# Second experts stage: the last unit's routing chain kept together, its counting behind more gates, and part of the third products ahead of the branch

## The chip, the cores and the metric

The kernel runs on one core of one Trainium2 chip. The metric is device time in microseconds (us) of one execution; lower is better. The times compared are medians of runs without a profile. The traces shown come from one profiled execution each. PE is the matrix engine (TensorE), DVE is VectorE, ACT is ScalarE, POOL is GpSimd, and SP is SyncE, which here only issues DMAs.

## The reference

Four residual stages in float32 on 1024 tokens of width 256. The change touches the fourth alone.

```python
x = x + layernorm(attention(layernorm(x)))        # 16 heads, softmax
x = x + layernorm(experts_0(layernorm(x)))        # 8 experts, all tokens
x = x + layernorm(attention_1(layernorm(x)))      # 16 heads, recurrent state
x = x + layernorm(experts_1(layernorm(x)))

def experts_1(x):                                 # 16 experts, top 4
    scores = softmax(x @ gate_weight.T)
    topk_weight, topk_idx = top_k(scores, 4)
    y = 0
    for e in range(16):
        w_e = sum(where(topk_idx == e, topk_weight, 0.0), axis=-1)
        y = y + w_e[:, None] * glu(x, gate_up[e], down[e])      # hidden 176
    return y + glu(x, shared_gate_up, shared_down)              # hidden 352

def glu(x, gate_up, down):
    g, u = split(x @ gate_up.T)
    return silu(g) * u @ down.T
```

## The kernel before

The last stage runs from about 1000 us to the end. It computes 13 of the 16 experts sparsely (on the tokens routed to them) and the last three, together with the shared network, densely (on all tokens, weighted by routing weights that are zero where a token did not choose them).

*Dense part.* The hidden units of the shared network and of the three dense experts are cut into seven tiles of up to 128. `gates(i, hf, part)` computes tile `i` for half `hf` of the tokens (512), or for a quarter of them (`early`, `late`): `gated` issues the matmuls `pg` and `pu` on PE (L828), the Silu `sg` on ACT (L830) and the product `mid` on DVE (L831). Five of the seven tiles hold hidden units of the dense experts; `weighted(hf)` multiplies those with the routing weights (DVE, L1683). `spreads()` prepares these weights: PE transposes `pt` (L1613), ACT copies, a write to DRAM, and broadcast loads on SP's queue (L1623). `down(products(hf), part)` forms the third products (`po`, L846) for the half, or for one pair of its 128-token blocks ("part 1" or "part 2"), and ACT copies or DVE adds them into `acc` (L856, L853).

*Routing.* `routed(u)` is a generator in three steps for the units of 2, 2 and 4 blocks of tokens:
1. logits `pl` on PE (L1513), and then on DVE, with one exponential on ACT, the softmax and the choice of four experts: `top` (L1518) to `chosen` (L1539) and `counts` (L1544).
2. counting: matmuls `pr` on PE (L1551 to L1557) number the tokens of each expert, and DVE makes row numbers of them: `at` (L1561) to `place` (L1569).
3. in the same step POOL issues four indirect DMAs (L1575) for each block, which scatter the tokens' rows `hrow` into `slots` in DRAM.

The program writes the order of PE's work by hand as a list of calls: a `next(units[u])` issues the next step of a unit's routing between two `gates`. The framework's scheduler places DVE's, ACT's and POOL's instructions around that, by costs of its own; `self.pinned` (a wrapper of `keep_in_program_order`) holds an instruction to the order in which the program issues it.

Before, the list behind the first quarters is: `gates(4, 0)`, logits of unit 2, `gates(5, 0)`, `gates(6, 0)`, counting of unit 2, `gates(0, 1)`, `spreads()`, `gates(1, 1)`, `crowded()`, `gates(2..6, 1)`. `crowded()` counts the tokens per expert (`pc`, L1591); if some expert has more than the slots hold, the kernel branches to a dense way (`to_all`, not taken with these inputs), otherwise to `to_slots`.

*Sparse part.* `to_slots` loops over 13 experts. `fetch(e)` loads the rows `xs` from `slots` (SP, L1716). `turn(e)` transposes them on PE (`pt`, L1723), copies the halves to `xT` on ACT (L1728) and DVE (L1730), and copies out the routing weight `share` (L1735) and the token number `number` (L1736), from a pool `mk` of four buffers. `middle(e)` runs gate and up (`pe`, L1702, with Silu on ACT, L1692, products on DVE, L1693). `out(e)` runs the third product (`po`, L1755), scales it by `share` on ACT (`ys`, L1760), and POOL adds it to `sums` in DRAM by an indirect DMA (L1765) with `number` as its index. Along the loop run the `weighted` products (issued at e = 3 and 4, though the scheduler placed them right behind the branch) and the eight `shift` adds to the residual (ACT, L319).

*Tail.* Before `out(12)` comes part 1 of `products(0)`; behind it, while the last sums are scattered and loaded back, part 2 of `products(0)` and both parts of `products(1)`: 84 matmul records. The last function adds the sums to `acc` (L1829), normalizes (L1839 to L1852) and stores.

All matmul results in this stage share one pool of eight PSUM buffers (`ps`, tag `b1`).

Of the kernel before, what the change touches and what calls it, by code (L numbers as in the profile page):

```python
# [10 lines left out]
AF = mybir.ActivationFunctionType  # L11
# [4 lines left out]
P = 128  # L16
T = 1024
TT = T // P
HALF = 512
# [44 lines left out]
class Net:  # L64
# [145 lines left out]
    def pinned(self, ins):  # L210

        return self.tc.keep_in_program_order(ins)

    def turning(self, ps, tp, acc=None):


# [90 lines left out]
    def shifted(self):  # L307

        nc = self.nc
        lost = self.route.tile([P, 3, TT], F32, name="lost")  # L310
        shift = self.route.tile([P, TT], F32, name="shift")
        nc.gpsimd.tensor_tensor(lost, self.mvs[:, :, :, 0], self.rss, ALU.mult)
        nc.gpsimd.tensor_tensor(shift, lost[:, 0, :], lost[:, 1, :], ALU.add)
        nc.gpsimd.tensor_tensor(shift, shift, lost[:, 2, :], ALU.add)
        nc.gpsimd.tensor_scalar(shift, shift, -1.0, None, ALU.mult)

        def add(tt):
            x = self.x[:, tt, :]
            nc.scalar.activation(x, x, AF.Identity, bias=shift[:, tt : tt + 1])  # L319

        return add

# [491 lines left out]
        self.nc.sync.dma_start(out=d, in_=w)  # L814
        return d

    def gated(self, ps, tmp, wg, wu, mid, m, hf, part=None):

        nc = self.nc
        part = part or slice(0, HALF)  # L820
        n = part.stop - part.start
        c = slice(hf * HALF + part.start, hf * HALF + part.stop)
        mid = mid[:, part]
        pg = ps.tile([m, n], F32, tag="b1", name="pg")
        pu = ps.tile([m, n], F32, tag="b1", name="pu")
        for w, p in ((wg, pg), (wu, pu)):
            for k in range(KC):
                nc.tensor.matmul(p, w(k), self.hT[:, k, c], start=(k == 0), stop=(k == KC - 1))  # L828
        sg = tmp.tile([m, n], F32, tag="sg", name="sg")
        nc.scalar.activation(sg, pg, AF.Silu)  # L830
        nc.vector.tensor_tensor(mid, sg, pu, ALU.mult)  # L831

    def down(self, ps, pieces, first, hf=None, then=None, more=None, part=None):

# [558 lines left out]
    def ways(self):  # L1393
# [4 lines left out]
        def new(name, *shape, dtype=F32):  # L1398
            return self.route.tile([P, *shape], dtype, name=name)

        self.hrow = new("hrow", TT, XR)
        self.earlier, self.ones = new("earlier", P), new("ones", P)
        self.nothing = new("nothing", 1)
        self.base = new("base", E1)
        self.blank = new("blank", CT, XR)
        self.slots = self.dram.tile([SLOTS, XR], F32, name="slots")
# [38 lines left out]
    def experts1(self):  # L1445
        nc, tc, a = self.nc, self.tc, self.a
        with ExitStack() as ctx:

            def pool(name, bufs, **more):
                return ctx.enter_context(tc.tile_pool(name=name, reuse_waits="tile", bufs=bufs, **more))  # L1450
# [2 lines left out]
            sw, xsp, tp_, sp, small = (  # L1453
                pool("d_sw", 1), pool("d_xs", 3), pool("d_xt", 2), pool("d_s", 3), pool("d_small", 2)
            )
            mk = pool("d_mk", 4)
            ps = pool("d_ps", 8, space=PSUM)

            wr = one.tile([P, KC, E1], F32, name="wr")
            nc.sync.dma_start(out=wr, in_=a["e1_wrT"].rearrange("(k p) e -> p k e", p=P))  # L1460
            rems = [one.tile([P, CAP], F32, name=f"rem_{i}") for i in range(3)]
            for r in rems:
                nc.gpsimd.memset(r, 0.0)
# [35 lines left out]
            def routed(u):  # L1499

                begin, N = UNITS[u]
                n = slice(begin, begin + N)
                sh = [P, N, E1]

# [10 lines left out]
                            start=(k == 0), stop=(k == KC - 1),  # L1515
                        )
                top, tot = new("top", 1), new("tot", 1)
                nc.vector.tensor_reduce(top, pl, AX.X, ALU.max)  # L1518
                nc.vector.tensor_tensor(v, pl, top.to_broadcast(sh), ALU.subtract)
                nc.scalar.activation(v, v, AF.Exp)  # L1520
                nc.vector.tensor_reduce(tot, v, AX.X, ALU.add)
                nc.vector.reciprocal(tot, tot)
                nc.vector.tensor_tensor(v, v, tot.to_broadcast(sh), ALU.mult)

                top8 = new("top8", 8)
                for i in range(N):
                    nc.vector.max(top8[:, i, :], v[:, i, :])
                least = top8[:, :, TOP1 - 1 : TOP1].to_broadcast(sh)
                eq, nth, more = new("eq", E1), new("nth", E1), new("more", 1)
                nc.vector.tensor_tensor(c, v, least, ALU.is_gt)  # L1530
                nc.vector.tensor_tensor(eq, v, least, ALU.is_equal)
                nc.vector.tensor_reduce(more, c, AX.X, ALU.add)
                nc.vector.tensor_tensor_scan(
                    nth.rearrange("p t n -> p (t n)"), within[:, n, :].rearrange("p t n -> p (t n)"),
                    eq.rearrange("p t n -> p (t n)"), 0.0, ALU.mult, ALU.add,
                )
                nc.vector.tensor_tensor(nth, nth, more.to_broadcast(sh), ALU.add)
                nc.vector.scalar_tensor_tensor(eq, nth, float(TOP1), eq, ALU.is_le, ALU.mult)
                nc.vector.tensor_tensor(c, c, eq, ALU.add)  # L1539
                nc.vector.tensor_tensor(  # L1540
                    self.hrow[:, n, XW : XW + SP1], v[:, :, 0:SP1], c[:, :, 0:SP1], ALU.mult
                )
                nc.vector.tensor_tensor(v[:, :, SP1:], v[:, :, SP1:], c[:, :, SP1:], ALU.mult)
                nc.vector.tensor_reduce(  # L1544
                    counts[:, u, :], c.rearrange("p t e -> p e t"), AX.X, ALU.add
                )
                yield
# [8 lines left out]
                for i in range(1, N):  # L1556
# [1 line left out]
                        pr[:, i:N, :], self.ones, c[:, 0 : N - i, :], start=False, stop=(i == N - 1)  # L1558
                    )
                at = new("at", SP1)  # L1560
                nc.vector.scalar_tensor_tensor(  # L1561
                    at, pr[:, :, 0:SP1], -1.0,
                    self.base[:, 0:SP1].unsqueeze(1).to_broadcast([P, N, SP1]), ALU.mult, ALU.add,
                )
                nc.vector.tensor_tensor(at, at, c[:, :, 0:SP1], ALU.mult)
                first = new("first", 8)
                for i in range(N):
                    nc.vector.max(first[:, i, :], at[:, i, :])
                nc.vector.tensor_scalar(  # L1569
                    place[:, n, :], first[:, :, 0:TOP1], -1.0, float(SPARE), ALU.mult, ALU.add  # L1570
                )
                for i in range(N):
# [69 lines left out]
                midp.tile([P, FP // P, HALF], F32, name=f"mid_{hf}") for hf in range(2)  # L1642
            ]

            def gates(i, hf, part=None):
                wg, wu, right, m, lo = tiles[i]
                self.gated(ps, tmp, wg, wu, mids[hf][0:m, i, :], m, hf, part)

            quarters = (slice(0, HALF // 2), slice(HALF // 2, HALF))
            units = [routed(u) for u in range(len(UNITS))]  # L1650
# [14 lines left out]
            group(1)  # L1665
            gates(FG1, 0)
            next(units[2])
            for i in range(FG1 + 1, len(tiles)):
                gates(i, 0)
            next(units[2])  # L1670
            gates(0, 1)
            spreads()
            gates(1, 1)
            full = crowded()
            for i in range(2, len(tiles)):
                gates(i, 1)
            shift = self.shifted()

            def weighted(hf):
                for i, (wg, wu, right, m, lo) in enumerate(tiles):  # L1680
                    if lo in spread:
                        v = mids[hf][0:m, i, :]
                        nc.vector.tensor_tensor(  # L1683
                            v, v, spread[lo][0:m, hf * HALF : (hf + 1) * HALF], ALU.mult
                        )

            def products(hf):
                return [(mids[hf][0:m, i, :], right) for i, (wg, wu, right, m, lo) in enumerate(tiles)]


            def silu_times(g, pg, pu, mid):
# [19 lines left out]
            def to_slots():  # L1711
# [6 lines left out]
                def turn(e):  # L1718
# [13 lines left out]
                    share = mk.tile([CP, CT, 1], F32, tag="share", name="share")  # L1732
                    number = mk.tile([CP, CT, 1], I32, tag="number", name="number")
                    xs = rows.pop(e)
                    nc.vector.tensor_copy(share, xs[:, :, XW + e : XW + e + 1])  # L1735
                    nc.vector.tensor_copy(number, xs[:, :, XID : XID + 1].bitcast(I32))  # L1736
                    marks[e] = share, number

                def middle(e):
# [43 lines left out]
                for e in range(SP1):  # L1783
                    if e + 1 < SP1:
                        turn(e + 1)
                    if e + 3 < SP1:
                        fetch(e + 3)
                    if e == SP1 - 1:
                        out(e - 1)
                    middle(e)  # L1790
                    if 0 < e < SP1 - 1:
                        out(e - 1)
                    if e in (3, 4):
                        weighted(e - 3)
                    if 0 <= e - 3 < TT:
                        shift(e - 3)
                    if e > 0 and e % S3 == 0 and (e // S3 + 1) * S3 < SP1:
                        load(e // S3 + 1)
                self.down(ps, products(0), True, 0, None, None, 1)
                out(SP1 - 1)  # L1800


# [19 lines left out]
                def plus(dst, x, y):  # L1822
                    nc.vector.tensor_tensor(dst, x, y, ALU.add)
# [36 lines left out]
                        nc.sync.dma_start(out=outv[:, tt, :], in_=x[:, tt, :])  # L1860

                p0, p1, p2, p3 = pairs
                plus(acc[:, p0, :], acc[:, p0, :], other[:, p0, :])
                self.down(ps, products(0), True, 0, None, other, 2)
                plus(acc[:, p0, :], acc[:, p0, :], got[:, p0, :])
                stats(0)
                plus(acc[:, p1, :], acc[:, p1, :], got[:, p1, :])
# [16 lines left out]
            def to_all():  # L1884
                for tt in range(TT):
                    shift(tt)
                for hf in range(2):
                    weighted(hf)
                    self.down(ps, products(hf), True, hf)
                for e in range(SP1):  # L1890
                    if e % S3 == 0 and e >= 2 * S3:
                        load(e // S3)
# [117 lines left out]
```

## Time and profile before

| what | us |
|---|---|
| three timed runs | 1192.67, 1192.94, 1194.61 (median 1192.94) |
| profiled execution, its own time | 1203.99 |
| its span (first to last instruction) | 1202.3 |
| PE busy in the span | 1124.2 (94%) |
| DVE busy | 707.3 (59%) |
| ACT busy | 519.5 (43%) |
| POOL busy | 222.6 (19%) |
| mean granted PE clock | 0.983 of full |
| last stage | about 1000 to 1202 |
| scatters of units 0 and 1 | 1017.9 to 1038.3 |
| scatters of unit 2 | 1049.4 to 1069.6 |
| loop over the 13 experts | about 1075 to 1174.5 |

In the lines of the profile a letter L and a number give the line of the kernel file. A line of the timeline has start, duration, engine, line, operation and the number of instructions, and in brackets the idle time ahead with the instruction that ended it. A matmul record is one pass of PE; a float32 matmul leaves two of them.

### The profile page before, as it was taken

What the parts mean: (1) busy time and instruction counts of PE and PEld (TensorE: products, weight loads), DVE (VectorE), ACT (ScalarE), POOL (GpSimd) and SP (SyncE); (2) the same over time, 40 slices, a digit from 0 to 9 for tenths busy, and PEclk for the clock granted to TensorE, in tenths of its full rate; (3) what the DMA queues carried; (4) which work ended last, traced back from release to release, by engine and by line L of the source; (5) the groups of instructions that cost most, each with busy time, mean ns of one, the idle gap of its engine ahead of it and who ended that gap; (6) DMA issues with size and microseconds to landing.
All of it is one profiled execution on the core that took longest, in us unless ns stands there. A gap on an engine that the chain in (4) does not pass through costs nothing. (4 is left out here: it accounts for less than half of the span.)

```text
span 1202.3 us, 15820 instructions
## 1 busy us (share of the span) xinstructions
PE 1124.2 (94%) x6002; PEld 688.6 (57%) x6002; DVE 707.3 (59%) x1682; ACT 519.5 (43%) x975; POOL 222.6 (19%) x209
## 2 busy tenths in 40 slices
PE   6999999998999999789999999999999987789996
PEld 3543333332457566356767676766676776447775
DVE  5876767761534335577677777777676857233224
ACT  4266666667131111445444454544444444223331
POOL 3100000000100000111111112121212124444662
PEclk9999999999999999999999999999999998899999
DMA  6000000000005101211313131222212114154844
GB/s 207 1 1 1 1 2 1 1 1 1 1 1 194 53 1 44 68 51 36 114 43 92 65 93 64 85 72 63 77 53 86 37 64 178 55 171 123 203 45 115
DMA packets 53495, 77.01 MB, mean 64 GB/s; under 512 B 7209, under 2 KB 44408, under 8 KB 53414
## 3 DMA queue, kind: packets, MB, share of 16 engines
q1 hardware_dynamic: 46886, 69.02, 18.0%
q0 software_dynamic: 6528, 6.93, 3.1%
q8 instruction: 49, 0.80, 0.3%
q14 instruction: 32, 0.26, 0.1%
HBM read 60.93 MB, written 17.00 MB: 65 GB/s over the span
## 5 line engine op out<-in xcount | busy, mean ns | idle before, releaser
L506 DVE TENSOR_REDUCE pm<-sc 128x1 f32<-128x512 f32 x256 | 163.2, 685 | 64.5 <-PE sc L570 43.2
L570 PE MATMUL sc<-qTm,kT 32*128 32x512 f32 x512 | 151.5, 644 | 1.9 <-ACT pe L588 1.9
L599 ACT ACTIVATE pe<-sc 128x512 f32<-128x512 f32 x216 | 117.8, 595 | 67.8 <-PE sc L570 47.3
L1155 ACT ACTIVATE sn<-pt,shift,rs 128x128 f32<-128x128 f32 x256 | 93.7, 470 | 106.9 <-DVE shift L1151 106.9
L501 PE MATMUL sc<-kT,qT 32*128 32x512 f32 x512 | 136.2, 637 | 1.6 <-ACT qT L460 0.8
L1115 PE MATMUL px<-hT,w_l1a 128*128 128x512 f32 x256 | 125.0, 600 | 5.4 <-DVE y L1107 5.1
L1107 DVE SCALAR_TENSOR_TENSOR y<-px,cp,y 128x1023 f32<-128x1023 f32 (+5 forms) x102 | 123.4, 1213 | 3.9 <-ACT y L1101 3.8
L1150 POOL TENSOR_TENSOR rs<-ve,nhalf 128x8 f32<-128x8 f32 x32 | 52.4, 1637 | 304.7 <-DVE ve L1149 249.9
L831 DVE TENSOR_TENSOR mid<-sg,pu 128x512 f32<-128x512 f32 (+1 forms) x50 | 32.0, 642 | 117.3 <-PE pu L828 100.8
L830 ACT ACTIVATE sg<-pg 128x512 f32<-128x512 f32 (+1 forms) x50 | 27.7, 562 | 134.2 <-PE pg L828 116.9
L232 POOL TENSOR_TENSOR rss<-ve,nhalf 128x2 f32<-128x2 f32 x12 | 8.4, 699 | 406.2 <-DVE ve L231 401.4
L557 PE MATMUL po<-pe,va 128*32 128x256 f32 (+1 forms) x872 | 79.6, 432 | 1.3 <-ACT oT L562 0.8
L570 PEld LDWEIGHTS sc<-qTm,kT 32*128 32x128 f32 x512 | 49.6, 184 | 54.3 <-issue 38.6
L1219 PE MATMUL pg<-hT,w_l1a 128*128 128x512 f32 x128 | 62.0, 610 | 9.8 <-DVE og L1335 8.2
L1765 POOL DMA_INDIRECT sums<-ys,number x39 | 57.3, 1470 | 53.0 <-ACT ys L1760 44.8
L557 PEld LDWEIGHTS po<-pe,va 128*32 128x32 f32 x872 | 17.9, 108 | 85.3 <-issue 75.5
L1115 PEld LDWEIGHTS px<-hT,w_l1a 128*128 128x128 f32 x256 | 44.0, 195 | 32.6 <-issue 30.7
L828 PE MATMUL pg<-hT,w_l0f 128*128 128x512 f32 x128 | 61.9, 605 | 0.0
L1125 ACT ACTIVATE y<-y 128x1024 f32<-128x1024 f32 x32 | 34.2, 1068 | 63.0 <-DVE y L1107 54.5
L1185 PE MATMUL pv<-w_l1a,hT 128*128 128x256 f32 x256 | 59.9, 382 | 1.4 <-DVE state L1319 0.7
L828 PE MATMUL pu<-hT,w_l0f 128*128 128x512 f32 x128 | 60.5, 594 | 0.0
L1136 DVE BATCH_NORM_STATS2 st<-pt 128x6 f32<-128x128 f32 x256 | 55.1, 283 | 5.3 <-PE pt L1134 5.3
(277 smaller groups left out, 2051.1 us busy)
## 6 DMA issues: line engine op xcount, KB each, us to landing
spread<-rows SPq DMA_DIRECT2D x32, 512.0 KB
sw<-in_e_s SPq DMA_DIRECT2D x4, 1872.0 KB
slots<-blank SPq DMA_DIRECT2D x13, 357.0 KB
xs<-slots SPq DMA_DIRECT2D x13, 357.0 KB
w<-w SPq DMA_DIRECT2D x9, 512.0 KB
w_l0f<-in_e_wg SPq DMA_DIRECT2D x4, 512.0 KB
w_l0f<-in_e_wu SPq DMA_DIRECT2D x4, 512.0 KB
w_l0f<-in_e_wd SPq DMA_DIRECT2D x4, 512.0 KB
```

The costliest lines, as they stand in the source:

```text
L501: nc.tensor.matmul(sc, raw[r, tt * P : (tt + 1) * P], kT[r, g, half(kh)], start=True, stop=True,)
L506: nc.vector.tensor_reduce(pm[:, tt, 2 * pair + i, kh : kh + 1], sc, AX.X, ALU.max)
L557: nc.tensor.matmul(po[0][rows(j), c], va[:, st, g * G + j, :], pe[j // 2][:, j % 2, c], start=(st == 0), stop=(st == TT - 1 and c.stop == ...
L570: nc.tensor.matmul(sc, kT[rows(j), g, st * P : (st + 1) * P], qm[rows(j), :], start=True, stop=True,)
L599: nc.scalar.activation(pe[pair][:, i, :], sc, AF.Exp, scale=scale)
L828: nc.tensor.matmul(p, w(k), self.hT[:, k, c], start=(k == 0), stop=(k == KC - 1))
L1107: nc.vector.scalar_tensor_tensor(y[:, at:hi], px[:, at - j : hi - j], column(cw + 4 * h + 3 - j), y[:, at:hi], ALU.mult, ALU.add,)
L1115: nc.tensor.matmul(px[:, c], w[:, k, hh * DK : (hh + 1) * DK], self.hT[:, k, c], start=(k == 0), stop=(k == KC - 1),)
L1155: nc.scalar.activation(sn[:, n, :], pts[n // 4][:, n % 4, :], AF.Identity, scale=rs[:, n : n + 1], bias=shift[:, n : n + 1],)
L1185: nc.tensor.matmul(pv[:, i, :, :].rearrange("p h v -> p (h v)"), self.hT[:, k, (n + i) * P : (n + i + 1) * P], wv[:, k, :], start=(k == 0) ...
L1219: nc.tensor.matmul(pg, wg[:, k, hh * DK : (hh + 1) * DK], self.hT[:, k, c], start=(k == 0), stop=(k == KC - 1),)
L1765: sent = nc.gpsimd.indirect_dma_start(out=self.sums[e % 2][:, :], out_offset=bass.IndirectOffsetOnAxis(ap=number[:, i, :].bitcast(U32), axis=0
```

## The change

- `wr`, the router's weights, is loaded at the start of the third stage instead of at the start of the fourth.
- `vector(pinned)` gives DVE's interface with every instruction pinned. The last unit's routing (u = 2) uses it, and so do the `mid`s of four gates around it.
- The counting of unit 2 is issued behind `gates(0, 1)` and the early quarter of `gates(1, 1)`; before, it stood ahead of both.
- `weighted(0)` is issued ahead of the last gate before the branch, and part 1 of `products(0)` behind that gate, still ahead of the branch. `weighted(1)` is pinned at e = 4.
- Part 2 of `products(0)` is issued ahead of `out(12)`, where part 1 stood; behind `out(12)` only `products(1)` is left.
- `share` and `number` are pinned behind the expert's `xT` copies, and `mk` has six buffers, not four.
- The `shift` adds are pinned, one per expert.

```diff
+    def vector(self, pinned):
+        vector, keep = self.nc.vector, self.pinned
+        class Pinned:
+            def __getattr__(self, name):
+                return lambda *args, **more: keep(getattr(vector, name)(*args, **more))
+        return Pinned() if pinned else vector
...
-            nc.scalar.activation(x, x, AF.Identity, bias=shift[:, tt : tt + 1])
+            self.pinned(nc.scalar.activation(x, x, AF.Identity, bias=shift[:, tt : tt + 1]))
...
-        nc.vector.tensor_tensor(mid, sg, pu, ALU.mult)
+        self.vector(pinned).tensor_tensor(mid, sg, pu, ALU.mult)
...
+        self.wr = new("wr", KC, E1)
+        nc.sync.dma_start(out=self.wr, in_=self.a["e1_wrT"].rearrange("(k p) e -> p k e", p=P))
...
-            mk = pool("d_mk", 4)
+            mk = pool("d_mk", 6)
...
             def routed(u):
+                vector = self.vector(u == len(UNITS) - 1)
...
-                nc.vector.tensor_reduce(top, pl, AX.X, ALU.max)
+                vector.tensor_reduce(top, pl, AX.X, ALU.max)
...
             gates(FG1, 0)
             next(units[2])
             for i in range(FG1 + 1, len(tiles)):
-                gates(i, 0)
+                gates(i, 0, None, True)
+            gates(0, 1, None, True)
+            gates(1, 1, early, True)
             next(units[2])
-            gates(0, 1)
+            gates(1, 1, late)
             spreads()
-            gates(1, 1)
+            gates(2, 1)
             full = crowded()
-            for i in range(2, len(tiles)):
+            for i in range(3, len(tiles) - 1):
                 gates(i, 1)
+            weighted(0)
+            gates(len(tiles) - 1, 1)
             shift = self.shifted()
+            self.down(ps, products(0), True, 0, None, None, 1)
...
-                    nc.vector.tensor_copy(share, xs[:, :, XW + e : XW + e + 1])
-                    nc.vector.tensor_copy(number, xs[:, :, XID : XID + 1].bitcast(I32))
+                    self.pinned(nc.vector.tensor_copy(share, xs[:, :, XW + e : XW + e + 1]))
+                    self.pinned(
+                        nc.vector.tensor_copy(number, xs[:, :, XID : XID + 1].bitcast(I32))
+                    )
...
-                    if e in (3, 4):
-                        weighted(e - 3)
+                    if e == 4:
+                        weighted(1)
...
-                self.down(ps, products(0), True, 0, None, None, 1)
+                self.down(ps, products(0), True, 0, None, None, 2)
                 out(SP1 - 1)
...
                 p0, p1, p2, p3 = pairs
-                plus(acc[:, p0, :], acc[:, p0, :], other[:, p0, :])
-                self.down(ps, products(0), True, 0, None, other, 2)
+                for p in (p0, p1):
+                    plus(acc[:, p, :], acc[:, p, :], other[:, p, :])
```

## The prediction

> **What bounds the kernel now.** I read the page's first two parts, then the waits, the timelines and the windows of the last stage (1000 us to the end), the only stage whose instructions differ between the built orders of the two kernels. TensorE (PE) is busy 94% of the span, so a change pays only where PE stands still, where its clock is low, or in the tail.
>
> ```profile
> span 1202.3 us, 15820 instructions
> PE 1124.2 (94%) x6002; PEld 688.6 (57%) x6002; DVE 707.3 (59%) x1682; ACT 519.5 (43%) x975; POOL 222.6 (19%) x209
> ```
>
> The waits between 1000 and 1110 us (total, times, longest) name PE's stops in this stage: the second units' counting, the first expert, and the start.
>
> ```profile
> PE pr L1551 <- DVE chosen L1539: 7.1, 2, 6.3
> PE pe L1702 <- DVE xT L1730: 3.5, 1, 3.5
> PE pt L280 <- ACT hrow L264: 3.5, 1, 3.5
> PE pl L1513 <- DMA wr<-in_e_wrT: 1.3, 1, 1.3
> DVE top L1518 <- remote: 7.8, 1, 7.8
> ```
>
> The timelines (start, duration, what; in brackets the idle time before) show the 6.3 us: the routing logits `pl` of the last unit are done at 29.81 + 1.71 = 1031.52, two gates run to 1038.49, and PE waits for `chosen`, since `top` began only at 1040.74.
>
> ```profile
> 1029.81 1.71 PE L1513 MATMUL pl<-wr,hT 128*128 128x16 f32 x14
> 1036.61 1.88 PE L828 MATMUL pu<-hT,w_l1f 128*128 128x512 f32 x4
> 1040.74 0.23 DVE L1518 TENSOR_REDUCE top<-pl 128x4 f32<-128x64 f32 x1 [7.76 <-remote]
> 1044.80 0.66 PE L1551 MATMUL pr<-chosen,earlier 128*128 128x64 f32 x2 [6.31 <-DVE chosen L1539]
> 1049.39 0.97 POOL L1575 DMA_INDIRECT slots<-hrow,place  x1 [11.06 <-issue]
> 1074.95 1.49 PE L1723 MATMUL pt<-ident,xs 112*128 112x112 f32 x12
> 1076.04 3.70 DVE L1683 TENSOR_TENSOR mid<-mid,w 128x512 f32<-128x512 f32 x6
> 1081.70 4.78 PE L1702 MATMUL pe<-xT,sw 128*128 128x336 f32 x10 [3.53 <-DVE xT L1730]
> ```
>
> The windows (granted clock behind the x-counts) show that the stop also costs speed:
>
> ```profile
> 1031.00:1041.00 10.00, 7.49 (x21) 3.31 (x20) 0.92 (x3) 0.29 (x1) 5.80 (x6) 1.00 0.21 75
> 1041.00:1051.00 10.00, 6.21 (x17) 4.17 (x18) 5.17 (x27) 2.62 (x4) 1.30 (x2) 0.50 0.02 6
> ```
>
> **Is that stop in the timed runs?** The profiled execution took 1203.99 us by its own time (span 1202.3 and 1.7 around it); the timed median is 1192.94, which is 11.05 less. VectorE (DVE) was idle for 7.76 us with its input computed nine microseconds before; the signal reached it 2.4 us after POOL's last scatter of the earlier units (1038.33). Suppose that in a timed run signals arrive at once, as elsewhere in this trace. Then `chosen` is ready by 1044.66 - 7.77 = 1036.9, before PE wants it at 1038.49. The 2.71 us of `pr` (1044.80 to 1047.51 at clock 0.5) are 1.36, to 1039.85; `place` follows 1.12 later (1048.63 - 1047.51), the first scatter 0.76 behind that, at 1041.7; the 16 scatters last 20.17 (to 1069.56 in the trace), and the first expert's transposes `pt` came 5.39 after them: 1067.3, not 1074.95. PE's own gates end at 1075.11 less 6.31 idle and half of the 6.46 us worked at half clock: 1065.6. The weighted products L1683 began 0.93 after that end and the full `pe` 5.66 after them: 1072.2, not 1081.70, 9.5 us earlier; and if the ten `pe` there are warm (2.84 by 12 in 3.41, not 4.78), 11.5. The 11.05 lies between. So I take it that the long stop belongs to the profiled execution and hardly to the timed ones. This is an inference, no row shows a timed run. The Trainium skill ("Runtime: NRT & Kernel Launch", the preamble and postamble breakdown) gives a fixed gap of about 6.2 us between a profile's total and the reported execution time; by it only some 4.9 us would be left for held signals, and part of the stop would be real.
>
> **The change, part by part, on the timed schedule just built.**
>
> *Start.* The early `wr` removes 1.25 us of waiting before the first `pl`, of which some 0.6 is left once hT's copy ends (1003.17 against 1003.79). But in the built order unit 0's `top` now stands on DVE right behind the statistics ending at 1003.87, where it waits for `pl` (ends near 1005.15): 1.28 us, and the next pairs' statistics, their `hrow` and PE's transposes queue behind it. I take +1.1 for all that follows; bounds -0.6 and +1.3. On SP the load is one issue, hidden in the attention stage.
>
> *The chain and the count.* Pinning takes one `mid` (0.6) out of `top` to `counts`; PE has no wait there in timed runs, so nothing. `pr` stands behind one and a half more gates: 3.43 + 1.72 = 5.15 us. `at` on DVE queues behind four pinned `mid`s, done 0.9 after their gates, inside `pr`'s 1.36. The scatters, SP's fetch of the slots and `pt` start 5.15 + 1.1 later: 1073.5 against 1067.3. POOL's earlier 16 are over by about 1039, so they hide nothing.
>
> *What gives it back.* Half 0's five weighted products (5 x 0.615 = 3.1 on DVE) and the 14 products of one pair (28 records; the same unit of L846 took 6.04) now come before the branch. PE's gates end at 1066.7 (+1.1), the products at 1072.7, so PE idles 0.8 before `pt` at 1073.5; 1.49 later `pe` of expert 0 can run, 12 records take 3.41, and expert 2's `pt` is at 1078.4. Before, `pe` starts whole at 1072.2, because ten weighted products sit ahead of DVE's xT copy, and has ten records left (2.84): expert 2's `pt` at 1075.0. That is +3.4. If before's clock also drops there (4.78, not 2.84), 1076.9 and +1.5. In the profiled clock rows the drop came at 1041.0, after 2.5 us of idle; before's gap between 1065.6 and 1072.2 holds 2.3 us of PE work. The Trainium skill ("TensorE: Matmul & The Clock Gate", Part 1) says that a whole idle window of about 3.4 us is needed; by the rule before stays warm (+3.4), by the row it may go cold (+1.5). The 11.05 is nearer to the warm sum.
>
> *Experts and tail.* Part 1 in front is paid back by part 2 in front of `out(12)`, so `out(12)` keeps its distance. The six marks remove `number`'s waits on the scatters (DVE 36.6 us in all after 1086, nearly all in DVE's slack); on PE three expert periods were 7.01, 6.66 and 7.09 against 6.57: 0 to 1.0, taken as 0.5. PE after `out(12)` falls from 84 records to 56, but the last add waited only 0.30 us for PE: DVE's chain from the gathered sums (1184.69) fills the rest, so the tail gives 0.3. The shift adds and weighted(1) move within ACT's and DVE's slack: nothing; uncovered, 0.45 and 0.6 each.
>
> Sum: +3.4 (or +1.5) - 0.5 - 0.3 = +2.6 (or +0.7). I take +2.3, nearer to warm: 1195.2. With the bounds of the start (-1.7 or +0.2 against my 1.1), of the marks, and up to 0.9 for the first xT copy, this case runs from -1.5 to +4.2: 1191.4 to 1197.2.
>
> **Rivals.**
> 1. *The stop is real in timed runs.* For it: it is what the trace shows. Against: the 11.05. Then 5.15 us of the 6.31 idle are filled with gates, `place` is about where it was (a `mid` less and a warm `pr`, against +1.1), and the gain is at the first expert: no weighted half in front of xT, so `pe` up to 5.3 + 1.9 us (cold) earlier, or only 1 if half 0's weighting waits for a `mid` whose signal is late as well (1072.08 in the trace). With 0.8 from the rest: -1.8 to -8; middle 1188.
> 2. *The count's delay is paid in full* (slower). Place: `pr` to the first `pe`. It decides as soon as the slots arrive after PE's own work (1073.5 against 1072.7 above) and before's DVE does not stand in the way of xT, so that before's `pe` starts 2.4 us after `pt` as in the trace's first two records: 1069.7, expert 2 at 1073.1. Against it: ten weighted products in the order. Price 5.3, less 0.8: 1197.4, and up to 1198.2.
> 3. *It does not do what it says:* the products ahead fill a hole and the tail stays set by the last scatter. That is part of my sum (0.3).
>
> **Chances.** My case 0.55, rival 1 0.32, rival 2 0.13. A measurement of this kernel tells 0.2%, 2.4 us. My case lies on that bound: half of it slower, nearly half within, a little faster. Rival 1 is three quarters faster, rival 2 slower. Together: faster 0.27, same 0.31, slower 0.42. The range, 1187 to 1198.2, leaves out the far end of rival 1 and little else; my case alone has 1191.4 to 1197.2.
>
> **What would show it.** In the profile after, the stop before `pr` should shrink to about a microsecond and PE run gates there; the first scatter should start about where it did (1049.4), while the profiled time falls by 2 to 8 us although the timed median doesn't: that split is the sign of held signals. The 28 records of `po` should lie before the branch, no L1683 between `pt` and the first xT copy, 56 records after `out(12)`, with the last add waiting for DVE's chain. `top` of unit 0 should wait over 1 us. A timed gain of over 2.4 us would say that the stop is real; a loss beyond 4.2, that before never paid for its weighted products.

## The result, and the profile after

The changed kernel takes 1196.25 us (median of 20 runs, 1194.58 to 1198.33), the kernel before 1193.88 (20 runs, 1192.48 to 1196.28): 1.002 times as long, 95% interval 1.0013 to 1.0027. The forecast was 1195.2. The profiled execution of the changed kernel took 1197.25 us by its own time, about its median; that of before, 1203.99, ten above its own. Profile against profile the change gains 6.7 us, run against run it loses 2.4.

The page's first lines of the changed kernel:

```profile
span 1195.5 us, 15834 instructions
PE 1122.0 (94%) x6010; PEld 689.7 (58%) x6010; DVE 706.0 (59%) x1683; ACT 520.5 (44%) x977; POOL 223.5 (19%) x209
```

PE's waits in the last stage (total, times, longest):

```profile
PE pt L290 <- ACT hrow L274: 3.5, 1, 3.5
PE pr L1563 <- DVE chosen L1551: 3.2, 1, 3.2
PE pt L1743 <- DMA xs<-slots: 1.9, 2, 1.4
PE pl L1525 <- ACT hT L291: 0.7, 1, 0.7
```

The wait for `wr` and that for `xT` are gone. A wait for `chosen` is there, but of unit 0, not of the last unit, and a new one for the slots. The timelines show the rest (most lines are now ten to some twenty further down, the weighted products are L1666, and L220 is the helper that pins):

```profile
1032.86 1.85 PE L1525 MATMUL pl<-wr,hT 128*128 128x16 f32 x16
1034.75 0.23 DVE L220 TENSOR_REDUCE top<-pl 128x4 f32<-128x64 f32 x1 [0.93 <-PE pl L1525]
1046.67 0.33 PE L1563 MATMUL pr<-chosen,earlier 128*128 128x64 f32 x2
1049.97 0.97 POOL L1587 DMA_INDIRECT slots<-hrow,place  x1 [10.07 <-ACT sg L840]
1068.45 6.21 PE L856 MATMUL po<-w_l1f,mid 128*128 128x256 f32 x28
1076.06 0.77 PE L1743 MATMUL pt<-ident,xs 112*128 112x112 f32 x6 [1.40 <-DMA xs<-slots]
1077.38 0.79 PE L1743 MATMUL pt<-ident,xs 112*128 112x112 f32 x6 [0.55 <-DMA xs<-slots]
1078.01 3.57 PE L1722 MATMUL pe<-xT,sw 128*128 128x336 f32 x12
```

`top` follows its logits within 0.04 us here, where the first profile of before had nine microseconds. PE runs without a gap from there to the end of the products. And it keeps its clock (the granted share of full speed, behind the x-counts) where before's profile had 0.50:

```profile
1031.00:1041.00 10.00, 10.00 (x36) 5.40 (x35) 4.59 (x21) 4.61 (x6) 6.83 (x7) 1.00 0.25 91
1041.00:1051.00 10.00, 10.00 (x47) 6.89 (x46) 3.22 (x11) 1.99 (x5) 0.97 (x1) 1.00 0.00 0
```

### The profile page after: what moved, and what is told of

It reads as the page before. It is cut to its first block, busy times and chain, and to the rows that moved or that the text cites. A ratio compares the mean times of both kernels' runs of the same rounds, so it can differ in the third digit from the quotient of the medians.

```text
span 1195.5 us, 15834 instructions
## 1 busy us (share of the span) xinstructions
PE 1122.0 (94%) x6010; PEld 689.7 (58%) x6010; DVE 706.0 (59%) x1683; ACT 520.5 (44%) x977; POOL 223.5 (19%) x209
```

## Experiments

**Two conditions.** The runs fell into two groups, which every number below depends on. In one, PE's signals arrive at once, and the kernel before takes 1193.0 to 1193.9 us (medians of four sets). In the other some of them arrive late while POOL issues the slot scatters, and it takes 1203.2 or 1203.0. Within one set of runs of before all belong to one group; the same chip showed both at different times. What sets it I did not find. I call them "at once" and "waiting". Each kernel is compared only with the runs of before in its own set. In brackets stand the labels of runs; b_ and a_ mean built from the kernel before and from the changed one.

The profiles tell the two apart without exception. In all six of the waiting condition the last unit's `top` starts 6.8 to 9.2 us after its logits, and always 2.3 to 2.5 us after the last scatter of the earlier units ends; in all eight of the other it starts 0.03 to 0.04 us after its logits. Not every signal is late: during unit 2's scatters the first `mid`s of each waiting profile follow their matmuls by 0.11 us, as at once, and later ones by up to 9.5 us.

| kernel | at once (us; ratio to before, 95%) | waiting |
|---|---|---|
| before | 1193.88, 1193.71, 1193.37, 1192.96 | 1203.24, 1202.97 |
| changed (the result) | 1196.25; 1.0020 (1.0013 to 1.0027) | not measured |
| the same again (a_again) | 1195.10; 1.0010 (1.000 to 1.002) | |
| the same again (a_third) | 1195.91; 1.0019 (1.0010 to 1.0028) | |
| the same again (a_fourth) | 1195.17; 1.0021 (1.0011 to 1.0031) | |
| before with chain and count only (b_count) | 1195.88; 1.0016 (1.0006 to 1.0026) | |
| changed, wr back | 1193.08; 0.9997 (0.9989 to 1.0006) | 1195.21; 0.9936 (0.9923 to 0.9950) |
| changed, count back | | 1200.54; 0.9974 (0.9965 to 0.9983) |
| changed, both back | 1191.91; 0.9985 (0.9977 to 0.9994) | 1201.84; 0.9985 (0.9976 to 0.9994) |
| changed, four marks | | 1201.59; 0.9988 (0.9972 to 1.0004) |

**The kernel before, profiled again.** No edit.

> The kernel before, unchanged, profiled once more. My theory: the late signals in the first profile of it (top waits 7.76 us, PE stops 6.31 us before pr, clock 0.5 for 10.24 us) belong to that one execution; here the profiled execution takes 1192.5 to 1196.5 us by its own time, top starts within 1 us of the last pl, PE stops for less than 1 us before pr of the last unit, and the transposes of expert 2 begin at about 1076.7. Rival (the stop is part of the kernel): again 1203 to 1204 us, top waits over 7 us, PE over 6.

It took 1204.55, and all 21 other runs of its set 1202.4 to 1205.3. So the rival was right in this set: the stop is real there, not a matter of one execution. The waits between 1000 and 1110 us repeat the first profile (PE's wait of 3.5 us for `xT` too):

```profile
DVE top L1518 <- remote: 9.1, 1, 9.1
PE pr L1551 <- DVE chosen L1539: 7.1, 2, 6.3
```

A third profile fell into the other condition.

> The kernel before, unchanged, profiled on whichever of the two kinds of chip this is. Where signals come at once (1192 to 1196 us by its own time) the schedule that the prediction built by hand should be seen: top within 1 us of the last pl, no stop before pr, first scatter of unit 2 at about 1041.7, transposes of expert 0 at 1067.3, full pe at 1072.2, transposes of expert 2 at 1075.0 if the clock stays up and 1076.9 if it drops. Where they wait: as in the two profiles of it so far, 1204.

1193.27 us. This is the schedule that the prediction had to build by hand:

```profile
1030.72 0.23 DVE L1518 TENSOR_REDUCE top<-pl 128x4 f32<-128x64 f32 x1 [0.93 <-PE pl L1513]
1037.48 0.33 PE L1551 MATMUL pr<-chosen,earlier 128*128 128x64 f32 x2
1040.78 0.97 POOL L1575 DMA_INDIRECT slots<-hrow,place  x1 [3.33 <-issue]
1065.50 3.70 DVE L1683 TENSOR_TENSOR mid<-mid,w 128x512 f32<-128x512 f32 x6
1065.83 0.77 PE L1723 MATMUL pt<-ident,xs 112*128 112x112 f32 x6 [1.26 <-DMA xs<-slots]
1071.16 4.76 PE L1702 MATMUL pe<-xT,sw 128*128 128x336 f32 x10 [1.91 <-DVE xT L1730]
1075.76 0.74 PE L1723 MATMUL pt<-ident,xs 112*128 112x112 f32 x6
```

and its window there, with a granted clock of 0.50:

```profile
1067.70:1074.50 6.80, 4.89 (x11) 2.70 (x10) 5.31 (x17) 0.89 (x2) 0.00 (x0) 0.50 0.38 108
```

Its last logits end 0.84 earlier than in the first profile (1030.68 against 1031.52). With that added: first scatter 1041.6 (built: 1041.7), `pt` 1066.7 (1067.3), full `pe` 1072.0 (1072.2), expert 2's `pt` 1076.6 (1075.0 warm, 1076.9 cold). The clock makes it the cold one.

**The changed kernel beside before, three more times.** No edit.

> The changed kernel itself, beside the kernel before on one chip. The runs so far show two kinds of measurement: one in which PE's signals wait while POOL scatters (before 1203.2 there) and one in which they come at once (before 1193.9). My theory: the change's sign hangs on that. Where before takes about 1203, the changed kernel takes 1195 to 1198, 0.994 to 0.996 of it, because gates now fill the stop before pr and the first expert's xT copy no longer waits for ten weighted products whose own inputs were signalled late; where before takes about 1194, it takes 1196 to 1197, 1.002. Rival (the loss of 0.2% is the change's own and the same everywhere): 1205.5 where before takes 1203.

> The changed kernel itself as the measure for the two beside it. Where signals come at once (before near 1194): 1195 to 1196.3, 1.001 to 1.002 of before. Where they wait (before near 1203): 1195 to 1198, since a_wr_back, which differs by its start alone, took 1195.2 there. Rival (the loss is the change's own everywhere): 1205.

> The changed kernel, to have it beside the kernel before on the chip that this is. Where signals wait (before near 1203): 1195 to 1198, 0.994 to 0.996 of before. Where they come at once: 1195 to 1196.3, 1.001 to 1.002. Rival (the loss is the change's own everywhere): 1205 where before takes 1203.

All three sets were at once: 1195.10, 1195.91, 1195.17 us, ratios in the table. The loss of 0.1 to 0.2% holds (the first set lies a little under the 1196 to 1197 expected for it). None fell into the waiting condition, so the changed kernel itself was not measured there. Three kernels that differ from it by one step were, at 0.9936, 0.9974 and 0.9988 of before (the last with an interval up to 1.0004), so the rival's 1205 is unlikely; but two of the three also miss the 1195 to 1198 expected of the changed kernel there.

**Only the pinned chain and the count behind more gates.** To before, parts of the edit:

```diff
             def routed(u):
+                vector = self.vector(u == len(UNITS) - 1)
...
             for i in range(FG1 + 1, len(tiles)):
-                gates(i, 0)
+                gates(i, 0, None, True)
+            gates(0, 1, None, True)
+            gates(1, 1, early, True)
             next(units[2])
-            gates(0, 1)
+            gates(1, 1, late)
             spreads()
-            gates(1, 1)
+            gates(2, 1)
...
```

> The kernel before with the pinned chain, the pinned mids and the counting behind one and a half more gates, and nothing else of the change: the weighted products, the products of the third layer, wr, the marks stay as before. My theory: where signals come at once it is slower, by 5.15 us of later slots less the 1.7 that PE idled and the weighted products hide: +1 to +2.5, 1195 to 1196.5 beside 1193.9. Where signals wait (before 1203), the stop of 6.3 us before pr and the half clock behind it go, but the slots come when they did: -1 to -3. Rival (the late parts make the whole gain there): 1203, no change.

1195.88 beside 1193.71, ratio 1.0016, inside the 1195 to 1196.5 expected: the pinned chain and the count's new place by themselves cost about what the whole change does. PE's timeline shows what it pays for the later slots:

```profile
1072.09 2.56 PE L1737 MATMUL pt<-ident,xs 112*128 112x112 f32 x12 [6.32 <-DMA xs<-slots]
1074.43 4.05 PE L1716 MATMUL pe<-xT,sw 128*128 128x336 f32 x12
```

6.32 us of idle PE, and `pe` behind it at 4.05, not 3.57. DVE, for its part, had six of its ten weighted products done in the meantime, so the `xT` copies come in time and `pe` runs its 12 records in one piece.

**wr back at the start of the stage.** To the changed kernel:

```diff
-        self.wr = new("wr", KC, E1)
-        nc.sync.dma_start(out=self.wr, in_=self.a["e1_wrT"].rearrange("(k p) e -> p k e", p=P))
...
-            wr = self.wr
+            wr = one.tile([P, KC, E1], F32, name="wr")
+            nc.sync.dma_start(out=wr, in_=a["e1_wrT"].rearrange("(k p) e -> p k e", p=P))
```

> The changed kernel with wr loaded at the start of the fourth stage again, so that DVE's order at the start is that of before; all else stays. My theory: the early wr put unit 0's top in front of the statistics, PE stopped 3.24 us before pr and then ran 3.41 us at half clock, 2.8 us in all, and all of that lies on the chain to the slots: 1193.4 us, 2.8 less than the changed kernel, the first scatter 1.1 us earlier. Rival (the count behind the gates is the whole loss, the start is hidden): 1196 us, no change.

> The changed kernel with wr loaded at the start of the fourth stage again, measured once more, beside the changed kernel. Where signals come at once (before near 1194): the 3.24 us stop before the first pr and the 3.41 us of half clock behind it go, all on the chain to the slots: 2.8 less than the changed kernel, 1192.5, about 0.999 of before. Where they wait (before near 1203): 1195 as measured. Rival (the start is hidden behind PE's work in front of the branch): the same as the changed kernel.

At once 1193.08, beside 1195.91 for the changed kernel in the same set: 2.83 less, as expected. In the waiting condition 1195.21, 8.0 less than before. At once, the early `wr` is a loss by itself. The cause is seen in the changed kernel's timeline of the set (a_third), in the `pr` of wr back in the same set (third line, a_wr_back2), and in a_third's windows:

```profile
1003.93 0.19 DVE L1530 TENSOR_REDUCE top<-pl 128x2 f32<-128x32 f32 x1 [1.29 <-PE pl L1525]
1015.36 0.41 PE L1563 MATMUL pr<-chosen,earlier 128*128 128x32 f32 x2 [2.24 <-DVE chosen L1551]
1013.58 0.41 PE L1562 MATMUL pr<-chosen,earlier 128*128 128x32 f32 x2 [0.46 <-DVE chosen L1550]
```

```profile
1016.00:1019.30 3.30, 3.30 (x8) 2.59 (x9) 2.98 (x21) 1.97 (x3) 1.24 (x1) 0.50 0.00 0
```

DVE stands 1.29 us at unit 0's `top`; `chosen` comes late; PE stops 2.24 us before `pr` and then runs 3.41 us at half clock. With wr back PE stops 0.46 us there, and the clock in the same window (1016.00 to 1019.30) is 1.00.

**The count back where it was**, and **both back** (this edit and wr back; the pinned chain, the weighted products and the products ahead of the branch stay):

```diff
+            next(units[2])
             gates(0, 1, None, True)
-            gates(1, 1, early, True)
-            next(units[2])
-            gates(1, 1, late)
+            gates(1, 1)
```

> The changed kernel with the counting of the last unit right behind gates(5,0) and gates(6,0), where the kernel before had it; all else stays. My theory: the slots come 5.15 us earlier, but then PE's own work in front of the branch ends last (1074.5 in the trace of the changed kernel, where the transposes waited for the slots until 1076.06 and 1077.38), so only 1.6 to 1.9 us are won: 1194.4 us. Rival (the slots set the time alone): 5 us, 1191. Rival (they are hidden): no change, 1196.

> Both at once: wr back and the counting back, with the pinned chain, the weighted rows and the products ahead of the branch, and six marks. My theory: 2.8 and 1.8 add up, 1191.6 us, faster than the kernel before by about 2 us, 0.998 of it. Rival (nothing but the two moves differs from before that counts): 1193.9, the time before.

> wr and the counting both back, with the rest of the change kept. Where signals come at once: the slots are early, PE's own work in front of the branch, products included, ends about 2.8 earlier than in the changed kernel and is followed by the transposes without a wait: pe of expert 0 some 4 us earlier, 1191, about 0.9975 of before. Where they wait: 1201.8 as measured. Rival (nothing of the late parts counts): the time of before.

The first two (a_count_early, a_both) fell into the waiting condition, where their expectations, written for signals at once, do not apply: 1200.54 and 1201.84. The count back by itself was not measured at once. Where signals wait, the count's early place costs 6.6 us (1201.84 against 1195.21 for wr back alone), for `pr` stands again behind a late `top` (waits of a_both in that set):

```profile
DVE top L220 <- remote: 7.8, 1, 7.8
PE pr L1562 <- DVE chosen L220: 5.8, 1, 5.8
```

At once, both back take 1191.91, 1.2 less than wr back alone and 0.9985 (0.9977 to 0.9994) of before; 1191 was expected. PE goes from the products into the experts with 0.37 us of idle (a_both2):

```profile
1064.83 6.21 PE L856 MATMUL po<-w_l1f,mid 128*128 128x256 f32 x28
1070.87 1.32 PE L1741 MATMUL pt<-ident,xs 112*128 112x112 f32 x12
1072.55 3.66 PE L1720 MATMUL pe<-xT,sw 128*128 128x336 f32 x12 [0.37 <-ACT xT L1746]
```

This version beats both kernels in the condition of the result, and before in both conditions. Where the waiting condition is likely, wr back alone is the better choice: equal at once, 0.64% faster when signals wait (five runs).

**Four marks, not six.**

```diff
-            mk = pool("d_mk", 6)
+            mk = pool("d_mk", 4)
```

> The changed kernel with four marks buffers instead of six; all else stays. My theory: the marks are what removed the long expert periods. In all profiles of kernels with six the later periods are 6.57 us each; here two or three of them should be 6.8 to 7.2 again, 0.9 us in sum, and number should wait on the sums' scatters; 196.6 + 1000 where the changed kernel takes 1195.7, or, as a ratio, 0.0007 more than its 1.0010 to 1.0021 beside the kernel before. Rival (the pinning of share and number behind xT removed them): all periods 6.57, no change.

Waiting, so its time says nothing on the marks; but its profile does. From expert 1 to expert 11 every `pe` period is 6.57 us, as in all kernels with six, where the kernel before has one of 6.82 and one of 7.20 (b_third). `number` still waits for the scatters (5.4 us in all on DVE) and delays nobody. My theory is wrong: the buffers did not remove the long periods. b_count, which has four buffers and leaves `share` and `number` unpinned, has two of them (7.20 and 7.17). That leaves the order, `share` and `number` behind the `xT` copies; but the pinned shift adds and weighted(1) go with it in every run, so it is not shown by itself. The 12 runs of four marks, 1193.66 to 1205.95, also show how wide the waiting condition spreads this design:

```profile
1071.75 0.69 DVE L841 TENSOR_TENSOR mid<-sg,pu 128x512 f32<-128x512 f32 x1 [7.77 <-remote]
1072.36 3.09 DVE L1666 TENSOR_TENSOR mid<-mid,w 128x512 f32<-128x512 f32 x5
1073.10 7.00 PE L856 MATMUL po<-w_l1f,mid 128*128 128x256 f32 x24 [4.69 <-DVE mid L1666]
```

Here the signal for the gate ahead of the weighted rows is held: its matmuls end 7.64 us before this `mid` starts, and PE stops 4.69 us inside the products. In the waiting profile of wr back the same `mid` ran at 1062.96, 0.11 us after its matmuls, the weighted rows at 1063.56, and PE did not stop. Why this signal is late in one and not in the other stays open.

## Why the prediction was right, step by step

Two profiles at once, each counted in us from the start of the stage's first transposes (`pt` from `hrow`). Of the kernel before there is one at once; the other three of the changed kernel differ from a_third by at most 0.6 us in any row:

| event | before (b_third) | changed (a_third) | difference | forecast |
|---|---|---|---|---|
| last logits end | 30.80 | 32.92 | +2.1 | +1.1 |
| `pr` of the last unit | 37.59 | 44.88 | +7.3 | +6.25 |
| first scatter of unit 2 | 40.89 | 48.18 | +7.3 | +6.25 |
| last scatter ends | 61.03 | 69.32 | +8.3 | +6.25 |
| `pt` of expert 0 | 65.94 | 74.33 | +8.4 | +6.25 |
| `pt` of expert 2 | 75.87 | 79.88 | +4.0 | +3.4 warm, +1.5 cold |
| `out(12)` ends | 163.83 | 166.96 | +3.1 | +2.9 warm, +1.0 cold |
| last instruction | 186.62 | 188.82 | +2.2 | +2.6 warm, +0.7 cold |

- *Is the stop in the timed runs?* For the runs that gave the result, no, as forecast, and the schedule built by subtraction was met to within 0.6 us. But the reason was wrong: I put the late signals down to the profiled execution. They belong to a condition that whole sets of runs share (1203.24, 21 runs), and a profiled execution can be free of it (1193.27). So the 11.05 us lie between two conditions. The record has a span and a granted clock for every timed run too, so it cannot show what an execution without any measurement inside the chip would take. The Trainium skill ("Runtime: NRT & Kernel Launch", the preamble and postamble breakdown) gives a fixed gap of about 6.2 us between a profile's total and the reported time. No gap of that size shows here: the changed kernel's profiled execution took 1197.25 us by its own time, its span is 1195.5, its median 1196.25.
- *Start: mis-sized.* +1.1 with bounds -0.6 and +1.3; the profiles show +2.1 and taking `wr` back is worth 2.83. The 1.28 us stall of DVE was right (1.29). The step that failed is what follows it: a stop of PE of 2.24 to 3.24 us before unit 0's `pr`, and one window of 3.41 us at half clock behind it, 1.7 us of lost work, which the sum did not hold. That `pr` itself starts only 0.5 us later (15.22 against 14.71), so the half clock is most of the +2.1. The wait that the early load removes is not the same each time either: PE waited 1.2 to 1.3 us for `wr` in three profiles and 2.8 to 3.1 in five.
- *Count: right.* From the last logits to `pr` it grows from 6.79 to 11.96, by 5.17 (5.15 forecast), and all of it reaches the slots: the first scatter moves by as much as `pr` (+7.3). b_count, with the chain and the count alone, shows the loss.
- *A missing term.* The scatters of unit 2 take 21.1 us in place of 20.1. Two of them, which start while DVE weights half 0, last about 1.5 in place of 0.97 (POOL's timeline of a_third):

```profile
1064.93 1.45 POOL L1587 DMA_INDIRECT slots<-hrow,place  x1 [0.30 <-DVE mid L1666]
1066.68 1.50 POOL L1587 DMA_INDIRECT slots<-hrow,place  x1 [0.30 <-issue]
```

  In all six profiles in which scatters start during these five products two of them are longer (1.25 to 1.50); of the same unit's scatters in the other eight profiles none is. The single `mid` products, which read one input from PSUM, run beside other scatters and leave them at 0.97. I had moved the weighted rows under cover of the gates without asking what else ran there.
- *What gives it back: the mechanism right, the clock wrong.* Before does lose its time to weighted products in front of xT (eight of the ten, not all, stand ahead of the copy that `pe` waits for). I leaned to the warm sum; before is cold (0.50 from 1067.73 for 6.83 us), so that sum should have been +1.5. PE had stood still for 1.26 and 0.63 us and was working in between. The Trainium skill ("TensorE: Matmul & The Clock Gate", Part 1) asks for a whole idle window of about 3.4 us; these rows contradict it, and 2.24 us before unit 0's `pr` were enough as well. The length of the stops alone does not decide it: in a_third PE stood for 1.46 and 0.76 us in front of expert 0, and its clock stayed at 1.00 there. This error (-1.9) and the start's and the scatters' (+1.0 each) nearly cancel: +4.0 for +3.4. What is left lies at expert 0, where `pe` follows the first `pt` by 2.15 us, not 1.49, because the second half of the transposes waited for its slots as well. That the total was met (+2.3 forecast, +2.4 measured) is in good part luck.
- *Loop: within its bounds, wrong in cause.* 0.9 us (forecast 0.5 of at most 1.0), which is what before's two long periods hold (0.25 and 0.63); not by the marks, and by the pinned order as far as is known.
- *Tail: 0.9, forecast 0.3.* From the end of `out(12)` to the last instruction 22.79 before (in all three profiles), 21.86 after (22.0 to 22.2 in the other three). The late parts move the end a little more than the one wait of 0.30 us showed.
- *Rivals.* The first was real elsewhere, as far as neighbours of the changed kernel can tell: in the waiting condition four marks gains 1.4 (its interval reaches no change) and wr back 8.0, about the two ends of its -1.8 to -8, though wr back also lacks the loss at the start. In their profiles the difference is the one named, whether the last `mid` before the weighting is signalled in time. The second (5.3 us) did not come: before's `pe` does wait for xT (1.91 us).
- The sign named in advance, profiled time down by 2 to 8 while the median is not, was seen (-6.7). It comes from two profiles taken in different conditions and does not mean that a profile slows a kernel.

## What to carry to other kernels

If a profiled execution is about 1% off the median of the runs, look in it for inputs that were ready long before their consumer began, rebuild the schedule without that, and cost the change on both; here a neighbour of the change loses nothing on one and gains 8 us on the other. A load moved earlier can lose: the scheduler then put an instruction that was not yet ready in front of others on DVE, and DVE stood there for 1.29 us. A PE stop of two microseconds can cost more than itself (2.24 us, then 3.41 us at half clock); put that into the sum of every stop that a change makes or removes, as a possibility, for other stops left the clock at 1.00.

## What was not expected of the hardware

- PE's completions can reach other engines late while POOL issues indirect scatters back to back: in before's first profile `top` began 9.2 us after its logits were done, 2.4 us after the last scatter. This is in all six profiles of the waiting condition and in none of the eight at once; the same chip showed both. That the scatters hold the signals is read from this timing; no run leaves them out.
- PE's clock fell to half after stops of 2.24 and 3.24 us (for 3.41 us) and after 1.26 and 0.63 us with work in between (for 6.83 us); after 1.46 and 0.76 us it did not.
- A 0.97 us indirect scatter that starts while DVE runs its five 128x512 products, both inputs in SBUF, takes 1.25 to 1.50.
